# Three projections of a linear-attention layer by a seven-product scheme on quarters, one block ahead, on one Trainium2 core

## The chip, the core and the metric

The kernel runs on one core of one Trainium2 chip. The core has a matrix engine (TensorE, PE in the profile, with its weight loads as PEld), a vector engine (VectorE, DVE), a scalar engine (ScalarE, ACT), a general engine (GpSimd, POOL) and a queue that only issues DMAs (SyncE, SP). Each engine works through a list of instructions of its own, and they wait for each other by semaphores. Matrix products land in PSUM, which has eight banks of 128 partitions by 512 f32 numbers; everything else is in SBUF. The metric is device time in microseconds (us), lower is better. The time of the kernel before is 550.33 us, the median of three runs (549.09 to 550.42).

## The reference

The input x is 4 x 2048 tokens of 256 features in f32, so 8192 tokens. Two stages follow each other, each with a residual and a LayerNorm:

```python
Q = x @ W_q.T;  K = x @ W_k.T;  V = x @ W_v.T            # 256 x 256 weights
mask = where(i >= j, decay ** (i - j), 0)                # inside chunks of 32 tokens
S = einsum('bncd,bnkd->bnck', Qc, Kc) * mask             # per chunk, no softmax
O = einsum('bnck,bnkd->bncd', S, Vc)
x = layernorm(x + (sigmoid(x @ W_g.T) * O @ W_o.T + x))

gate = x @ wg.T;  up = x @ wu.T                          # int weights / 127, 768 hidden
x = layernorm(x + (silu(gate) * up) @ wd.T)
```

The attention part is computed in full f32. The FFN weights are integers from -127 to 127.

## The kernel before

The 8192 tokens are cut into 16 blocks of 512 (TB = 512, NB = 16). xT, the features by tokens, is loaded beside x, since a product needs its contraction on the partitions. `M = W_q.T W_k` is formed once (`make_m`), so that a block needs three projections of 256 x 256 before its attention, and none of K:

- `attn_y` (L314): y = M x, features by tokens, two PSUM banks, copied out by DVE (L327).
- `attn_gate` (L298): sigmoid(W_g x), features by tokens, two banks, ACT applies the sigmoid as it copies out (L311).
- `attn_v` (L330): v, tokens by features, two banks, copied out by ACT (L346).

Each of the three contracts 256 features in two steps (`ec`) and has two halves of output, so it is made of eight products of quarters. `attn_scores` (L351) forms y.T x in squares of 64 tokens and DVE multiplies the mask in (L369). `attn_values` (L374) multiplies v with the scores, and DVE multiplies the gate in (L387). `attn_out` (L421) projects back with W_o (the `pa` products, L406), adds 2x, and normalizes on DVE: `moments` (L264, L265), a square root on ACT (`root`, L273), then one pass over the tile (L288). The result h carries a factor of 2^23.

The FFN gets about f32 precision from two faster products: h is split into a high part in a reduced f32 type (`hT_hi`) and a low part in f16 (`hT_lo`). The integers are exact in both types; `integers` (L214) casts them on ACT into `fg_hi`, `fg_lo` and so on. `ffn_up` (L492) goes through hidden chunks `hc` of 128: eight products of 512 tokens into two banks (fg, fu), a sigmoid on ACT (L510), two multiplications on DVE (L512, L514), a cast to `u_hi` on ACT (L521), and the low part `u_lo` on POOL (L522). `ffn_down` (L524) makes the `fdn` products from `u_hi` and `u_lo`, and `finish` normalizes and stores.

h has to be transposed before the FFN. In the loop this is done off TensorE: `move_h` (L454) transposes squares of 32 on DVE (L461) and moves them with 16 DMAs on SP (L467); `split_h` (L475) then makes the high part on ACT (L484) and the low part on DVE (L485). The first and the last block are transposed on TensorE (`transpose_h`).

The loop runs over b = 0 to 13. One pass does the FFN of block b and the attention of block n = b + 2, and moves h of block b + 1. In source order a pass is: y, gate and v of n; scores; `move_h`; FFN chunks 0 to 2; values; `split_h`; chunks 3 to 5; `attn_out`; `ffn_down` and `finish`. Blocks 0 and 1 are done ahead of the loop, with y of block 2; the FFN of blocks 14 and 15 comes after it.

The order on each engine is set by a planner: it takes instructions in source order, but lets a later one pass when the earlier ones are not ready by its own cost estimates. `tc.keep_in_program_order` ties an instruction to its place. PSUM is one pool of eight banks (`bank`), and a bank comes free when its last reader is done. SBUF pools have a fixed number of buffers for each tag; `acts` has nine of `u_hi`.

Of the kernel before, what the change touches and what calls it, by code (L numbers as in the profile page):

```python
# [46 lines left out]
SQ = 32  # L50
TB = 512
NG = TB // P
SCALE = 1.0 / 127.0
EXACT = 128.0
H_UP = 2.0**23
# [6 lines left out]
def kernel(  # L62
# [28 lines left out]
    moved = ctx.enter_context(tc.tile_pool(name="moved", bufs=1))  # L91

    acts = ctx.enter_context(tc.tile_pool(name="acts", bufs=H // P + 3))
    small = ctx.enter_context(tc.tile_pool(name="small", bufs=8))
    psum = ctx.enter_context(tc.tile_pool(name="psum", bufs=8, space=bass.MemoryType.PSUM))

    def bank(name):
        return psum.tile([P, TB], F32, tag="ps", name=name)
# [36 lines left out]
    xns[0] = load_xn(0)  # L135
    if NB > 1:
        xns[1] = load_xn(1)
    ffn_int = [
        load_w(nc.sync, w, name)
        for w, name in ((ffn_gT, "fg_int"), (ffn_uT, "fu_int"), (ffn_dT, "fd_int"))  # L140
    ]


# [67 lines left out]
        nc.gpsimd.memset(sT, 0.0)  # L211


    def integers(w_int, name, dtype):  # L214
        name = f"{name}_{'hi' if dtype == F32R else 'lo'}"
        t = const.tile(list(w_int.shape), dtype, tag=name, name=name)
        tc.keep_in_program_order(nc.scalar.copy(t, w_int))
        return t


    halves = [
        (w_int, slice(i * w_int.shape[1] // 2, (i + 1) * w_int.shape[1] // 2))
        for w_int in ffn_int
        for i in range(2)
    ]
    top = const.tile([P, len(halves)], F32, tag="top", name="top")

    def look_up(i):
        w_int, ks = halves[i]
        reduced = nc.vector.tensor_reduce(  # L230
            top[:, i : i + 1],
            w_int[:, ks, :].rearrange("p k n -> p (k n)"),
            mybir.AxisListType.X,
            ALU.max,
            apply_absolute_value=True,
        )
        tc.keep_in_program_order(reduced)

    def count_wide():

        wide = const.tile([P, len(halves)], F32, tag="wide", name="wide")
        nc.vector.tensor_scalar(wide, top, EXACT, None, ALU.is_gt)
        ones = const.tile([P, 1], F32, tag="ones", name="ones")
        nc.vector.memset(ones, 1.0)
        pw = bank("pw")
        nc.tensor.matmul(pw[:1, : len(halves)], lhsT=ones, rhs=wide, start=True, stop=True)
        count = const.tile([1, 1], F32, tag="count", name="count")
        nc.vector.tensor_reduce(count, pw[:1, : len(halves)], mybir.AxisListType.X, ALU.add)
        n_wide = const.tile([1, 1], I32, tag="n_wide", name="n_wide")
        nc.vector.tensor_copy(n_wide, count)  # L250
        return n_wide
# [27 lines left out]
    def layer_norm(dst, r, name, on_r=1.0, on_dst=1.0):  # L279
# [7 lines left out]
        for g in range(NG):  # L287
# [6 lines left out]
                ALU.mult,  # L294
            )


    def attn_gate(b):  # L298
        xt = xTs[b]
# [90 lines left out]
    def back_terms(g, parts, ws):  # L390


        pairs = list(zip(parts, ws))[:: -1 if g % 2 else 1]
        return [(part[k], w[:, k, :]) for part, w in pairs for k in range(len(part))]

    def project_back(b, parts, ws, finish, name):

# [17 lines left out]
    def chunked(t):  # L415
        return [t[:, k, :] for k in range(t.shape[1])]
# [4 lines left out]
    def attn_out(b, goT, up=H_UP):  # L421
        xn = xns.pop(b)
        r = norm.tile([P, NG, D], F32, tag="h", name=f"h_{b}")

        def residual(gs, pb):

            nc.vector.scalar_tensor_tensor(
                flat(r, gs), flat(xn, gs), 2.0, pb, ALU.mult, ALU.add
            )

        project_back(b, (chunked(goT),), (wo,), residual, "pa")
        layer_norm(r, r, f"a{b}", on_dst=up)
        return r

# [40 lines left out]
    def split_h(b, hT):  # L475
        hi = work.tile([P, KD, TB], F32R, tag="hT_hi", name=f"hT_hi_{b}")
        lo = work.tile([P, KD, TB], F16, tag="hT_lo", name=f"hT_lo_{b}")
        for dc in range(KD):
            whole = hT[:, dc, :, :].rearrange("p q (g t) -> p g q t", g=NG)
            in_order = [  # L480
                part[:, dc, :].rearrange("p (g q t) -> p g q t", g=NG, q=NQ)
                for part in (hi, lo)
            ]
            tc.keep_in_program_order(nc.scalar.copy(in_order[0], whole))  # L484
            rest = nc.vector.tensor_tensor(  # L485
                in_order[1], whole, in_order[0].bitcast(F32), ALU.subtract
            )
            tc.keep_in_program_order(rest)
        return hi, lo


# [32 lines left out]
    def ffn_down(b, uT, h):  # L524
        r = work.tile([P, NG, D], F32, tag="r2", name=f"r2_{b}")

        def residual(gs, pb):

            nc.vector.scalar_tensor_tensor(
                flat(r, gs), pb, SCALE**3 / U_UP * H_UP, flat(h, gs), ALU.mult, ALU.add  # L530
            )

        project_back(b, uT, fd, residual, "fdn")
        return r

    def store(b, r, start=None):
# [23 lines left out]
    if second:  # L560
        sT_second = attn_scores(second, ys.pop(second))
    hs[first] = attn_out(first, goT, 1 if NB == 1 else H_UP)
    fg, fu = (
        [integers(w, name, dtype) for dtype in (F32R, F16)]
        for w, name in zip(ffn_int, ("fg", "fu"))
    )
    if second:
        goT = attn_values(second, sT_second, v_second, sg_second)
    if NB > 2:
        xTs[2] = load_xT(2)  # L570
        ys[2] = attn_y(2)
    if second:
        hs[second] = attn_out(second, goT, 1 if NB == 2 else H_UP)
    fd = [integers(ffn_int[2], "fd", dtype) for dtype in (F32R, F16)]
    hTs[first] = transpose_h(first, hs[first], 1 if NB == 1 else H_UP)


    half = range(KH // 2), range(KH // 2, KH)
    looked = 0
    for b in range(NB - 2):  # L580
        n = b + 2
        if n not in xTs:
            xTs[n] = load_xT(n)
        xns[n] = load_xn(n)
        hT = hTs.pop(b)
        uT = [], []
        yT = ys.pop(n) if n in ys else attn_y(n)
        sg, v = attn_gate(n), attn_v(n)
        sT = attn_scores(n, yT)
        moving = move_h(b + 1, hs[b + 1])  # L590
        ffn_up(b, hT, uT, half[0])
        goT = attn_values(n, sT, v, sg)
        hTs[b + 1] = split_h(b + 1, moving)
        ffn_up(b, hT, uT, half[1])
        hs[n] = attn_out(n, goT, 1 if n == NB - 1 else H_UP)
        finish(b, ffn_down(b, uT, hs.pop(b)))
        if looked < len(halves):
            look_up(looked)
            looked += 1
    for i in range(looked, len(halves)):  # L600
        look_up(i)


# [67 lines left out]

    for g in range(NG):
        pb = bank(f"fdn_{last}_{g}")[:, :D]
        terms = back_terms(g, uT_last, fd)
        for i, (part, w) in enumerate(terms):
            nc.tensor.matmul(
                pb,
                lhsT=part[:, g * P : (g + 1) * P],
                rhs=w,
                start=(i == 0),  # L680
                stop=(i == len(terms) - 1),
            )
        in_turn(
            nc.vector.scalar_tensor_tensor(
                r[:, g, :], pb, SCALE**3 / U_UP, hs[last][:, g, :], ALU.mult, ALU.add
            )
        )
        mv = moments(r, f"f{last}_{g}", [g], order=in_turn)
        if g == 0 and NB > 1:
            normalize(r_before, mv_before, std_before, f"f{last - 1}", H_UP)  # L690
            store(last - 1, r_before)
        std = root(mv, f"f{last}_{g}", groups=[g], order=in_turn)
        waiting.append((g, mv, std))
        if 0 < g < NG - 1:
            normalize_first()
        if g == NG - 2:
            normalize_first()
# [8 lines left out]
    def wide_block(start, weights):  # L706
# [18 lines left out]
        for hc in range(KH):  # L725
            pg = bank(f"fg_w_{hc}")
            pu = bank(f"fu_w_{hc}")
            for pb, w in ((pg, wide_g), (pu, wide_u)):
                for dc in range(KD):
                    nc.tensor.matmul(  # L730
                        pb,
                        lhsT=w[:, dc, hc * P : (hc + 1) * P],
                        rhs=hT[:, dc, :],
                        start=(dc == 0),
                        stop=(dc == KD - 1),
                    )
# [8 lines left out]
                flat(r, gs), pb, H_UP, flat(h, gs), ALU.mult, ALU.add  # L745
            )

        project_back("w", (uT,), (wide_d,), residual, "fdn")
        finish("w", r, start)

    wide_any = nc.values_load(
        n_wide, min_val=0, max_val=len(halves) * P, skip_runtime_bounds_check_because="a count"
    )
    with tc.If(wide_any > 0):
        weights = []
        for w_int in ffn_int:
            t = w_int.bitcast(F32)
            nc.vector.tensor_scalar(t, w_int, SCALE, None, ALU.mult)
            weights.append(t)
        with tc.For_i(0, NT, TB) as start:  # L760
            wide_block(start, weights)

# [41 lines left out]
```

## Time and profile before

The profile is of one execution with a span of 548.2 us, at a mean granted TensorE clock of 0.995.

| engine | busy us | share | instructions |
|---|---|---|---|
| PE | 538.8 | 98% | 3150 |
| PEld | 387.6 | 71% | 3150 |
| DVE | 385.3 | 70% | 956 |
| ACT | 231.3 | 42% | 383 |
| POOL | 128.6 | 23% | 122 |

PE, PEld, DVE, ACT and POOL are the engines; L12 is line 12 of the kernel. A group of instructions is named by its line, what it writes and what it reads. Ends of matrix products are modelled in the profile and overlap the next start, so their pace is read from start to start, or from the chain that ended last, which counts every stretch of time once. A product in full f32 shows as two records with a weight load each. "Idle before" is time in which an engine had nothing to do, with what ended it; it costs nothing on an engine that is not the bottleneck.

### The profile page before, as it was taken

The page shows a single profiled execution, that of the slowest core. Times are in us where ns is not written, and L with a number is a line of the kernel's source. Part 1 is how long each engine was busy: PE and PEld are TensorE (multiplying, and loading weights), DVE is VectorE, ACT ScalarE, POOL GpSimd, SP SyncE. Part 2 cuts the span into 40 slices and gives each one's busy share as a digit, 9 for nine tenths or more (in the row PEclk, how much of TensorE's full clock was granted, in tenths as well). Part 3 has the DMA queues.
Part 4 walks back from the last instruction along what each step waited for, and adds up shares of the span by engine and source line. Part 5 has one row for each costly group of instructions (what it writes and reads, how often), then busy time and mean ns, then how long its engine had stood idle before and what let it go on. Part 6 is the DMA issues. An engine that isn't in the chain of part 4 may idle for free.

```text
span 548.2 us, 8472 instructions
## 1 busy us (share of the span) xinstructions
PE 538.8 (98%) x3150; PEld 387.6 (71%) x3150; DVE 385.3 (70%) x956; ACT 231.3 (42%) x383; POOL 128.6 (23%) x122
## 2 busy tenths in 40 slices
PE   8999999999999999999999999999999999999994
PEld 5677767767667686677857677676676867678793
DVE  4267784859768486794848758496784858848875
ACT  2217524336243352433435243452433425344745
POOL 2000412305022040321304022050221404123453
PEclk9999999999999999999999999999999999999997
DMA  7431214121221312214122231213213120020102
GB/s 256 168 113 50 67 45 110 39 71 45 89 66 39 84 54 77 58 42 112 40 64 52 70 85 39 74 43 94 62 39 93 62 62 16 8 71 1 38 2 80
DMA packets 41996, 36.77 MB, mean 67 GB/s; under 512 B 4576, under 2 KB 37344, under 8 KB 41952
## 3 DMA queue, kind: packets, MB, share of 16 engines
q1 hardware_dynamic: 40832, 35.15, 22.5%
q10 hardware_dynamic: 1088, 1.05, 0.6%
q8 instruction: 26, 0.43, 0.3%
q14 instruction: 18, 0.15, 0.1%
q0 software_dynamic: 32, 0.00, 0.0%
HBM read 20.45 MB, written 8.39 MB: 53 GB/s over the span
## 4 chain that ended last, share of the span: by engine, by line
PE 97%; DVE 1%; ACT 1%; issue 0%; POOL 0%; DVEq 0%
PE fg L502 16%; PE fu L502 16%; PE fdn L406 15%; PE pg L304 10%; PE pa L406 10%; PE pv L339 10%; PE py L320 10%; PE po L380 5%; PE ps L359 3%; PE pi L148 1%; ACT r L646 0%; PE pt L443 0%; PE pm L162 0%; ACT L273 0%; ACT rstd_f L273 0%
## 5 line engine op out<-in xcount | busy, mean ns | idle before, releaser
L522 POOL TENSOR_TENSOR u_lo<-u,u_hi 128x512 f16<-128x512 f32 (+1 forms) x102 | 123.9, 1216 | 409.5 <-ACT u_hi L521 405.0
L510 ACT ACTIVATE s<-fg 128x512 f32<-128x512 f32 (+1 forms) x102 | 58.1, 570 | 76.2 <-PE fg L502 76.1
L512 DVE SCALAR_TENSOR_TENSOR s<-fg,s 128x512 f32<-128x512 f32 (+1 forms) x102 | 66.7, 654 | 28.0 <-ACT s L510 27.8
L521 ACT CAST u_hi<-u 128x512 fp32r<-128x512 f32 (+1 forms) x102 | 60.4, 592 | 48.8 <-DVE u L514 48.3
L514 DVE TENSOR_TENSOR u<-fu,s 128x512 f32<-128x512 f32 (+1 forms) x102 | 67.1, 660 | 13.8 <-POOL u_lo L522 1.1
L502 PE MATMUL fg<-hT_hi,fg_hi 128*128 128x512 f32 (+1 forms) x204 | 71.5, 431 | 0.0
L369 DVE TENSOR_TENSOR sT<-ps,mask 64x256 f32<-64x256 f32 x32 | 13.5, 422 | 78.5 <-PE ps L359 78.2
L502 PE MATMUL fu<-hT_hi,fu_hi 128*128 128x512 f32 (+1 forms) x204 | 61.4, 382 | 0.0
L502 PE MATMUL fg<-hT_lo,fg_lo 128*128 128x512 f16 (+1 forms) x204 | 58.9, 369 | 0.0
L304 PE MATMUL pg<-xT,wg 128*128 128x512 f32 x128 | 58.2, 598 | 0.0
L339 PEld LDWEIGHTS pv<-wv,xT 128*128 128x128 f32 x256 | 48.6, 190 | 13.4 <-issue 7.7
L502 PE MATMUL fu<-hT_lo,fu_lo 128*128 128x512 f16 (+1 forms) x204 | 58.1, 366 | 0.0
L406 PE MATMUL pa<-wo,goT 128*128 128x256 f32 x256 | 58.0, 379 | 0.0
L339 PE MATMUL pv<-wv,xT 128*128 128x256 f32 x256 | 57.9, 379 | 0.0
L320 PE MATMUL py<-xT,m_sb 128*128 128x512 f32 x128 | 57.6, 593 | 0.0
L406 PE MATMUL fdn<-fd_hi,u_hi 128*128 128x256 f32 x360 | 55.2, 295 | 0.0
L406 PEld LDWEIGHTS pa<-wo,goT 128*128 128x128 f32 x256 | 48.5, 190 | 7.6 <-DVE rstd_a L286 0.2
L406 PEld LDWEIGHTS fdn<-fd_hi,u_hi 128*128 128x128 f32 x360 | 46.6, 189 | 1.1
L304 PEld LDWEIGHTS pg<-xT,wg 128*128 128x128 f32 x128 | 24.4, 192 | 31.1 <-issue 28.9
L406 PE MATMUL fdn<-fd_lo,u_lo 128*128 128x256 f16 x360 | 44.5, 273 | 0.0
L502 PEld LDWEIGHTS fg<-hT_hi,fg_hi 128*128 128x128 f32 x204 | 36.6, 189 | 10.3
L502 PEld LDWEIGHTS fu<-hT_hi,fu_hi 128*128 128x128 f32 x204 | 37.5, 188 | 7.8
(91 smaller groups left out, 612.6 us busy)
## 6 DMA issues: line engine op xcount, KB each, us to landing
x<-in_x_dram SPq DMA_DIRECT2D x16, 512.0 KB, 3.5
xT<-in_xT_dram SPq DMA_DIRECT2D x15, 512.0 KB, 3.8
out_dram<-r SPq DMA_DIRECT2D x15, 512.0 KB, 3.3
hT<-sq SPq DMA_DIRECT2D x224, 32.0 KB, 1.9
fg_int<-in_ffn_gT_dram SPq DMA_DIRECT2D x1, 768.0 KB, 9.5
fu_int<-in_ffn_uT_dram SPq DMA_DIRECT2D x1, 768.0 KB, 10.9
fd_int<-in_ffn_dT_dram SPq DMA_DIRECT2D x1, 768.0 KB, 10.4
xT<-in_xT_dram SPq DMA_DIRECT2D x2, 256.0 KB, 4.2
```

The lines of the kernel that those rows point to most:

```text
L304: nc.tensor.matmul(pg, lhsT=wg[:, ec, dc * P : (dc + 1) * P], rhs=xt[:, ec, :], start=(ec == 0), stop=(ec == KD - 1),)
L320: nc.tensor.matmul(py, lhsT=m_sb[:, ec, fc * P : (fc + 1) * P], rhs=xt[:, ec, :], start=(ec == 0), stop=(ec == KD - 1),)
L339: nc.tensor.matmul(pv[:, j * D : (j + 1) * D], lhsT=xt[:, ec, g * P : (g + 1) * P], rhs=wv[:, ec, :], start=(ec == 0), stop=(ec == KD - 1),)
L359: nc.tensor.matmul(ps[rows, g, :], lhsT=xt[:, fc, tokens], rhs=yT[:, fc, tokens], start=(fc == 0), stop=(fc == KD - 1),)
L380: nc.tensor.matmul(po[:, cols], lhsT=v[:, g, dc * P : (dc + 1) * P], rhs=sT[:, cols], start=True, stop=True,)
L406: nc.tensor.matmul(pb[:, j * D : (j + 1) * D], lhsT=part[:, g * P : (g + 1) * P], rhs=w, start=(i == 0), stop=(i == len(terms) - 1),)
L502: nc.tensor.matmul(pb, lhsT=w[kind][:, dc, hc * P : (hc + 1) * P], rhs=hT[kind][:, dc, cols], start=(kind == kinds[0] and dc == 0), stop=( ...
L510: nc.scalar.activation(s, pg, AF.Sigmoid, scale=SCALE / H_UP)
L512: nc.vector.scalar_tensor_tensor(s, pg, U_UP / H_UP**2, s, ALU.mult, ALU.mult)
L514: nc.vector.tensor_tensor(u, pu, s, ALU.mult)
L521: nc.scalar.copy(hi, u)
L522: nc.gpsimd.tensor_tensor(lo, u, hi.bitcast(F32), ALU.subtract)
```

## The change

For y, gate and v of blocks 3 to 15 the eight products of quarters are replaced by seven (a scheme of the Strassen and Winograd kind). The weight is cut into quarters of 128 x 128, the block's xT into quarters of 128 features x 256 tokens. `weight_sums` forms five sums of weight quarters on POOL once for each of the three weights; `token_sums` forms four sums of token quarters on POOL once for each block, used by all three projections.

`seven` works in two parts. The first part makes products 1, 5, 7 and 6 into four banks (half of each is used). ACT copies 1, 5 and 7 to SBUF, DVE adds 6 and the copy of 1 to `u`, and POOL adds the copies of 5 and 7 to `p57`. The second part, called later, adds products 2, 3 and 4 onto the banks of 1, 5 and 7, and forms the four quarters of the result: one by ACT, two by DVE (bank plus `u`), one by POOL (`p57` plus `u`). For the gate, ACT applies the sigmoid to the first quarter as it copies, and to the others in place afterwards. For v the token quarters are the stationary operand, in groups of 128 tokens.

In the loop a pass now makes the three projections of block m = b + 3, one block ahead, with a piece of the FFN between the parts:

```diff
-        yT = ys.pop(n) if n in ys else attn_y(n)
-        sg, v = attn_gate(n), attn_v(n)
+        yT, v, sg = ahead.pop(n)
+        ffn_up(b, hT, uT, range(0, 2))
         sT = attn_scores(n, yT)
+        if m is not None and m + 1 < NB:
+            xTs[m + 1] = load_xT(m + 1)
         moving = move_h(b + 1, hs[b + 1])
-        ffn_up(b, hT, uT, half[0])
+        ffn_up(b, hT, uT, range(2, 3))
+        v_rest = y_rest = g_rest = nothing
+        if m is not None:
+            v_next, v_rest = split_v(m, x_sums[m])
+        ffn_up(b, hT, uT, range(3, 4))
+        v_rest()
         goT = attn_values(n, sT, v, sg)
+        if m is not None:
+            y_next, y_rest = split_y(m, x_sums[m])
+        ffn_up(b, hT, uT, range(4, 5))
+        y_rest()
         hTs[b + 1] = split_h(b + 1, moving)
-        ffn_up(b, hT, uT, half[1])
+        ffn_up(b, hT, uT, range(5, KH))
+        if m is not None:
+            sg_next, g_rest = split_gate(m, x_sums.pop(m))
         hs[n] = attn_out(n, goT, 1 if n == NB - 1 else H_UP)
+        g_rest()
+        if m is not None:
+            ahead[m] = y_next, v_next, sg_next
+            if m + 1 < NB:
+                x_sums[m + 1] = token_sums(xTs[m + 1], f"x_{m + 1}")
         finish(b, ffn_down(b, uT, hs.pop(b)))
```

The core of the scheme:

```diff
+        banks = {i: bank(f"p{i}_{name}")[:, :HB] for i in (1, 5, 7, 6)}
+        p = {}
+        for i, pb in banks.items():
+            product(i, pb, True)
+            if i != 6:
+                p[i] = part(f"p{i}")
+                nc.scalar.copy(p[i], pb)
+        u = part("p6")
+        nc.vector.tensor_tensor(u, banks[6], p[1], ALU.add)
+        p57 = part("p57")
+        nc.gpsimd.tensor_tensor(p57, p[5], p[7], ALU.add)
+
+        def others():
+            for i, onto in ((2, 1), (3, 5), (4, 7)):
+                product(i, banks[onto], False)
+            c11, c12, c21, c22 = (quarter(i, j) for i in range(2) for j in range(2))
+            nc.scalar.activation(c11, shaped(banks[1], c11), func)
+            nc.vector.tensor_tensor(c12, shaped(banks[5], c12), shaped(u, c12), ALU.add)
+            nc.vector.tensor_tensor(c21, shaped(banks[7], c21), shaped(u, c21), ALU.add)
+            nc.gpsimd.tensor_tensor(c22, shaped(p57, c22), shaped(u, c22), ALU.add)
```

The other parts of the change:

- The low part of h in `split_h` goes from DVE to POOL, and is no longer tied to its place:

```diff
-            rest = nc.vector.tensor_tensor(
+            nc.gpsimd.tensor_tensor(
                 in_order[1], whole, in_order[0].bitcast(F32), ALU.subtract
             )
-            tc.keep_in_program_order(rest)
```

- y, gate and v of block 2 are made ahead of the loop by the old functions: v directly after y, gate after `attn_out` of block 1 and the casts of `fd`. Then come the weight sums, the load of xT and the token sums of block 3, and the transposes of h of block 0.
- The integer weights are loaded in nine pieces of 128 x 512, which lie in the nine `u_hi` buffers of the pool `acts`, and no longer in three tiles of their own. ACT casts them piece by piece, 18 casts in place of six. `look_up`, the check of the largest weight, reads the cast high parts. The branch for weights over 127, which this input doesn't take, loads them anew.

## The prediction

> **What bounds the kernel now.** I read the page's busy line and chain first, then the chain of one steady loop pass in order of time, then the windows of two passes, then the waits.
>
> The page:
>
> ```profile
> PE 538.8 (98%) x3150; PEld 387.6 (71%) x3150; DVE 385.3 (70%) x956; ACT 231.3 (42%) x383; POOL 128.6 (23%) x122
> ...
> PE 97%; DVE 1%; ACT 1%; issue 0%; POOL 0%; DVEq 0%
> ...
> L522 POOL TENSOR_TENSOR u_lo<-u,u_hi 128x512 f16<-128x512 f32 (+1 forms) x102 | 123.9, 1216 | 409.5 <-ACT u_hi L521 405.0
> ```
>
> 97% of the chain is TensorE. A busy PE need not be PE at its peak, so I looked at start-to-start times. The chain of one pass (start, us, what):
>
> ```profile
> 241.13 3.43 PE py L320 x8
> 244.56 3.44 PE pg L304 x8
> 248.00 3.45 PE pv L339 x16
> 251.45 1.08 PE ps L359 x32
> 252.53 0.66 PE fg L502 x2
> 253.19 0.47 PE fu L502 x2
> ...
> 258.15 1.78 PE po L380 x16
> 259.93 0.43 PE fg L502 x2
> ...
> 265.32 3.45 PE pa L406 x16
> 268.78 5.51 PE fdn L406 x48
> ```
>
> Each group begins where the last one ends: no gap. The three products that the change touches (y, gate, v) are 3.43 + 3.44 + 3.45 = 10.32 us of a pass. Windows of two passes (us, PE, PEld, DVE, ACT, POOL busy, clock, DMA share, GB/s):
>
> ```profile
> 240.97:274.13 33.16, 33.16 (x194) 23.69 (x193) 24.36 (x59) 13.44 (x22) 7.68 (x6) 1.00 0.23 64
> 274.13:307.25 33.12, 33.12 (x195) 23.69 (x194) 23.39 (x57) 13.44 (x22) 7.70 (x6) 1.00 0.23 65
> ```
>
> A pass is 33.1 us of PE at full clock, and every other engine has at least 8.8 us spare. PE's own waits are one line, before any work (PE pi on DVE idle, 1.5 us). So PE time taken out comes off the span, as long as no other engine's order makes PE wait.
>
> [...] py 3.43/8 = 429 ns for 512 columns, pv 3.45/16 = 216 ns for 256, po 1.78/16 = 111 ns for 128[...] Trace: u_lo takes 1280 ns at 512 elements and 731 at 256, 2.1 ns an element; and the one large DVE operation with two SBUF inputs, the low part of h, is bimodal (min/median/max):
>
> ```profile
> L485 DVE TENSOR_TENSOR hT_lo<-hT,hT_hi x28: 677/688/1375, 63.0 to 494.4; 128x512 f16<-128x512 f32 x28
> ```
>
> [...]
>
> **The change part by part.** It works on blocks 3 to 15, so 13 passes; block 2 keeps the old products and only moves ahead of the loop.
>
> *Seven products.* A quarter product is 128x128x256. For y and gate it is 2 records of 256 columns: 7 x 2 x 0.2156 = 3.02 us for 3.43 or 3.44. For v the weights move, in 2 groups of 128 columns: 7 x 2 x 2 = 28 records of 128 columns, at po's 0.111: 3.12 us for 3.45. Saved: 0.41 + 0.42 + 0.33 = 1.16 us a pass, 13 x 1.16 = 15.1 us. All of it is on the path. Bounds for v: 2.99 us at the pace of 256 columns; the other end stands under the rivals.
>
> *Two parts with an FFN chunk between.* New changes of kind on PE. In the chain the first fg pair after f32 products costs 0.66 against 0.47 when it begins with the high part (after ps) and 0.43 when it begins with the low part (after po). Chunk 3 and 5 begin low, chunk 4 high; scores now stand ahead of chunk 2 (high) as they stood ahead of chunk 0. So one more, 0.19 us a pass: 2.5 us (from 0 to 5).
>
> *Sums and evacuation.* Nearest rows are those at 128x256: ACT 380 to 405 ns, DVE 414 to 423, POOL 731. Per pass ACT gains 9 copies, 3 c11 and two sigmoids in place (0.38 + 0.60) and loses 4 at 0.59: +3.3 us, and 0 to 2 table loads more, since gate's sigmoids now stand between the two square roots: 13.4 becomes 16.7 to 19.3. DVE gains 9 x 0.42 = 3.8 and loses two y copies (1.3) and the low part of h (2.0): 24.4 becomes 24.9. POOL gains 4 token sums, 3 p57, 3 c22 (10 x 0.73) and two low parts (about 1.3 each; above that if the rearranged read costs more): 7.7 becomes 17.6. All are below the new pass of about 32.2 us, so throughput costs nothing; PE's work beside them hides them, if the waits below fit.
>
> *The waits.* New: the second part (p2 onto bank 1, p3 onto 5, p4 onto 7) waits for ACT's copies. For v the four first products take 4 x 0.445 = 1.78 us and chunk 3 follows with 1.83. p1's copy has from 0.45 to 3.6 us, p7's from 1.3 to 4.5. ACT must do in that time the copies (1.2), s and u_hi of chunk 2 (1.2), perhaps the u_hi before (0.6): 3.0 us. It fits with 0.6 us or more. For gate the cover is pa, 3.45 us. Queued behind the copies are s and u_hi of the next chunk; FFN banks wait for those.
>
> *Banks.* Three of eight are held through a chunk (1.8 + 1.8 + 1.3 us and the evacuation), so 5 remain for chunks (2 each, free 1.1 and 1.9 us after the chunk) and po. On DVE, the slack that stood beside y, gate and v (idle 4.9 us ahead of sT) is now later. In the first 8 us of a pass DVE owes the rest of the FFN norm (about 4.2), four transposes (1.7), sT (0.86), and s and u of three chunks (4.1), some 11 us; the backlog of 3 us leaves chunk 2's banks held until po, when 8 are wanted. I take 0.15 us a pass for both waits, 2 us (0 to 13).
>
> *h moved one place.* The transposed h goes out in DMAs whose issue is long (start, us; SP's queue):
>
> ```profile
> 244.91 1.87 SPq L467 DMA_DIRECT2D hT<-sq  x3
> 246.83 0.59 SPq L537 DMA_DIRECT2D out_dram<-r  x1
> 247.46 8.53 SPq L467 DMA_DIRECT2D hT<-sq  x13
> 256.09 0.53 SPq L109 DMA_DIRECT2D xT<-in_xT_dram  x1
> ```
>
> 16 issues are 10.4 us, 1.9 more to landing: 17 us after the pass begins. The load of xT now stands ahead of them (0.5 us), and waits for the scores at 4.8 us if SP keeps that order: landing at 17.5 to 18.5. split_h stands after y's second part, at about 18.3 us by PE. So ACT arrives as the data does; behind it wait s of chunk 5 and gate's copies, with pa to cover. The low part on POOL (2.6 us) is then done by 22 to 25 us; h is wanted at 32. Nothing, up to 0.5 us a pass.
>
> *Ahead of the loop.* Gate and v of block 2 stand ahead of the transposes of h, which came at 44.71; ffn_up(0) now follows these directly and waits for ACT, which has fd's casts (6 x 0.54), sigmoids and a table load nearby. 1 us (0 to 4). 15 POOL weight sums at about 0.4 us lie beside it. Casts in 18 pieces for 6: 9.7 for 8.2 us of ACT, hidden by the f32 products. Integer loads are 9 of 256 KB for 3 of 768 KB, used 25 us after landing.
>
> *Last pass.* It has no products of a block ahead: PE 22.8 us, DVE about 21. 1 us (0 to 4).
>
> Sum: -15.1 + 2.5 + 2 + 1 + 1 = -8.6; 548.2 - 8.6 = 539.6 us of span. The median of the three runs, 550.33, is 2.1 above that span: **541.7 us**.
>
> **The rivals.**
> 1. *PE waits for copies or banks* half a microsecond more each pass: 13 x 0.5 = 6.5, 548.2 us: still just faster or level. For: ACT's u_hi waits for DVE in 68 places already (48.3 us), and what is listed behind it waits too. Against: the margins above, and ACT at most 60% busy.
> 2. *ACT's queue held at the high part of h*, the slower end. If the transposes run after sT (about 9.7 us) instead of in DVE's gaps, h lands at about 22 us; s of chunk 5 and gate's copies wait 3 us behind it, u_lo of chunk 5 comes at 27.4 plus POOL's queue, and fdn stands from 26.6. 1.5 us of PE a pass: 541.7 + 19.5 = 561. It decides from about 0.8 us a pass ((552 - 541.7)/13). Against: in this trace the transposes run at 1 to 4 us, interleaved with the norm, though the source has them after the scores.
> 3. *v is limited by weight loads*: 28 f32 loads of 190 ns one after another are 5.3 us, 1.9 more than now, 13 x 2.2 = 28 us above the forecast. po speaks against it: same loads at 192 ns, 16 records in 1.78 us. I give it almost nothing.
> 4. *The change doesn't do what it says*: an eighth of 10.32 us is 1.29, and 1.16 remains; the record count shows it.
>
> **How the numbers follow.** Forecast, its own range 537.5 to 545.5: 0.60. Better than it (no waits, no switch cost: 548.2 - 15.1 + 2.1 = 535 is the floor): 0.05. Rival 1, up to 548.7: 0.13; its end that reaches no change, 548.7 to 552.0 (0.3% either way, about what a measurement can tell): 0.08. Rivals 2 and 3, slower: 0.14. So faster 0.78, same 0.08, slower 0.14. The range of 8 in 10 runs from 536.5 to 551.
>
> **What would show it.** Right: passes of 32.3 us; v's first and second part 1.78 and 1.33 us; 14, 14 and 28 records; PE at 97% of the chain; POOL near 250 us; low part of h near 1.3 us. Wrong: PE waits on ACT copies ahead of the second parts, or on DVE for a bank, of over 0.8 us a pass; hT_hi waiting for the DMA of hT; v's records at 120 ns or more.

## The result and the profile after

The kernel after takes **545.58 us** (median of four runs, 545.20 to 547.08), beside 550.38 for the kernel before (four runs, 549.09 to 551.12). The ratio is 0.992, with a 95% interval of 0.9894 to 0.9947: faster by 0.8%. The forecast of 541.7 was 3.9 us too low. The 545.58 lies 0.08 us above the forecast's own range (537.5 to 545.5) and inside the range of 8 in 10 (536.5 to 551). The kernel before, run beside the later experiments too, had medians of 550.34 (experiments 1 to 4) and 550.43 (5 to 8), so times of different experiments can be compared. The profiled execution of the kernel after was the longest of its four: a span of 545.3 us, where the other three have 543.4 to 544.0. The sums below are made from its trace and so end on that span.

The page after, with the lines that answer to those shown of before:

```profile
PE 527.8 (97%) x3462; PEld 419.8 (77%) x3462; DVE 387.7 (71%) x1019; ACT 306.9 (56%) x551; POOL 261.1 (48%) x295
...
PEclk9999799999999999999999999999999999999998
...
PE 90%; DVE 3%; ACT 2%; SPq 1%; POOL 1%; issue 1%; DMA 0%; DVEq 0%; ACTq 0%
...
L677 POOL TENSOR_TENSOR u_lo<-u,u_hi 128x512 f16<-128x512 f32 (+1 forms) x102 | 123.7, 1214 | 173.4 <-ACT u_hi L676 172.3
L641 POOL TENSOR_TENSOR hT_lo<-hT,hT_hi 128x512 f16<-128x512 f32 x28 | 35.3, 1282 | 27.6 <-ACT hT_hi L640 27.6
```

TensorE's busy time fell by 11.0 us (538.8 to 527.8), but its share of the chain fell from 97% to 90%. The chain now leaves TensorE at two more places: from 48.8 to 56.9, ahead of the loop, and from 468.9 to 497.0, where it follows h of block 14 (its norm, its DMAs, its two parts) to the end of the last pass. Most of that second stretch lies beside busy TensorE, so the share is no measure of time lost; the waits are. The row of granted clock has a single 7, early on. PE's waits (engine, line, awaited; us in total, times, longest); the line left out is that of before, pi on DVE:

```profile
PE fg L657 <- ACT hT_hi L602: 3.8, 1, 3.8
PE fdn L562 <- POOL u_lo L677: 1.8, 1, 1.8
...
PE fdn L562 <- ACT u_hi L676: 0.6, 1, 0.6
```

Each new wait occurs once, not thirteen times. The first stands at the start of the first FFN chunk of pass 0, the other two in the last pass, which makes no products of a block ahead. The chain of a pass that does, from 283.78 to 315.77 (start, us, what; 288.46 follows the scores):

```profile
288.46 0.66 PE fg L657 x2
...
290.48 1.78 PE p_v L380 x16
292.26 0.43 PE fg L657 x2
...
294.04 1.34 PE p_v L380 x12
...
297.17 1.73 PE p_y L364 x8
298.89 0.46 PE fg L657 x2
...
300.70 1.29 PE p_y L364 x6
...
303.79 1.73 PE p_g L364 x8
...
308.97 1.29 PE p_g L364 x6
```

v is 1.78 + 1.34, y and the gate are 1.73 + 1.29 each: 9.16 us for 10.32 before, 1.16 less. The second parts of v and y begin where the FFN chunk ends, that of the gate where `pa` ends. Windows of two passes, and of the place with the 7 (us; PE, PEld, DVE, ACT, POOL busy; clock; DMA share; GB/s):

```profile
91.74:123.75 32.01, 32.01 (x218) 26.07 (x217) 24.35 (x63) 18.97 (x34) 17.20 (x18) 1.00 0.24 66
123.75:155.76 32.01, 32.01 (x217) 26.07 (x217) 24.46 (x63) 19.09 (x34) 17.18 (x18) 1.00 0.23 67
56.80:62.40 5.60, 5.51 (x13) 2.69 (x14) 2.67 (x4) 1.12 (x3) 0.00 (x0) 0.51 0.24 51
```

A pass is 32.01 us for 33.13. The third window holds chunk 0 of the first block's FFN and most of chunk 1 (13 products; a chunk has eight): TensorE is busy all through it, at half clock.

**Where the time went**, from the spans (548.2 to 545.3):

| stretch | before | after | difference |
|---|---|---|---|
| ahead of the loop and pass 0, to the end of the first `fdn`, without y, gate and v of block 3 | 75.47 | 91.74 - 9.16 = 82.58 | +7.1 |
| the twelve passes that follow, and the 1.16 us saved in the thirteenth | 12 x 33.13 | 12 x 32.01 | -13.4 - 1.2 = -14.6 |
| last pass, b = 13, without products of a block ahead | 33.15 - 10.32 = 22.83 | 25.66 | +2.8 |
| from there to the end | | | +1.9 |

The last line is in the stores. From the end of the last pass to the end of DVE's last operation both traces have the same 39.02 us; then the issues of the last four stores took 3.45 us for 2.84, and from issue to landing they took 3.0 for 1.8 (median). From the end of DVE's last operation to the end of the span are 2.9 us before, 4.9 after and 5.0 in experiment 1 (533.40 to 538.4); no run shows why. The sum is -2.8 for -2.9.

**The +7.1.** ACT's timeline ahead of the loop, after (start, us, instruction, count, in brackets the idle time before it):

```profile
50.54 0.30 ACT L305 ACTIVATE rstd_a<-mv_a,eps 128x4 f32<-128x4 f32 x1 [4.11 <-DVE mv_a L297]
50.75 1.64 ACT L253 CAST fd_hi<-fd_int 128x512 fp32r<-128x512 int32 x3
...
53.97 1.28 ACT L467 ACT_TABLE_LOAD   x1
55.26 1.08 ACT L467 ACTIVATE sg<-pg 128x512 f32<-128x512 f32 x2
56.23 1.09 ACT L602 ACTIVATE hT_hi<-pt 128x512 fp32r<-128x512 f32 x2
```

TensorE's transposes of h of block 0 begin at 52.05 and last a microsecond. Their evacuation `hT_hi` stands on ACT behind the square root of block 1's norm, six casts of fd, a table load and two sigmoids of the gate. ACT idles 4.11 us ahead of that square root. Before, `hT_hi` ran ahead of it:

```profile
45.35 1.08 ACT L446 ACTIVATE hT_hi<-pt 128x512 fp32r<-128x512 f32 x2 [1.08 <-PE pt L443]
47.17 0.30 ACT L273 ACTIVATE rstd_a<-mv_a,eps 128x4 f32<-128x4 f32 x1 [0.73 <-DVE mv_a L265]
```

So TensorE waits 3.8 us, and what follows runs at half clock (0.51 in the window from 56.80). Some 0.4 us of the 7.1 lie earlier, in the first projection of the kernel (4.68 us in the chain for 4.22).

**The +2.8.** ACT's and then PE's timeline in the last pass:

```profile
492.57 1.14 ACT L640 CAST hT_hi<-hT 128x512 fp32r<-128x512 f32 x2 [2.16 <-DMA hT<-sq]
```

```profile
494.28 0.38 PE L562 MATMUL fdn<-fd_hi,u_hi 128*128 128x256 f32 x1 [0.62 <-ACT u_hi L676]
...
497.04 0.94 PE L562 MATMUL fdn<-fd_lo,u_lo 128*128 128x256 f16 x7 [1.81 <-POOL u_lo L677]
```

ACT stands at the high part of h until the DMA of hT has landed; `u_hi` of the last chunk is behind it (at 493.62), and on POOL `u_lo` behind two low parts of h (2.5 us). In a pass with products this is hidden: in the one shown ACT waited 0.47 us for the landing, at 302.03, and TensorE still had pa and the gate's second part to do.

### The profile page after: what moved, and what is told of

Its sections match the earlier page's. It is cut to its first block, busy times and chain, and to the rows that moved or that the text cites. A ratio compares the mean times of both kernels' runs of the same rounds, so it can differ in the third digit from the quotient of the medians.

```text
span 545.3 us, 9852 instructions
## 1 busy us (share of the span) xinstructions
PE 527.8 (97%) x3462; PEld 419.8 (77%) x3462; DVE 387.7 (71%) x1019; ACT 306.9 (56%) x551; POOL 261.1 (48%) x295
## 4 chain that ended last, share of the span: by engine, by line
PE 90%; DVE 3%; ACT 2%; SPq 1%; POOL 1%; issue 1%; DMA 0%; DVEq 0%; ACTq 0%
PE fg L657 16%; PE fu L657 15%; PE fdn L562 14%; PE pa L562 10%; PE p_v L380 7%; PE p_y L364 7%; PE p_g L364 7%; PE po L536 5%; PE ps L515 3%; PE py L476 2%; PE pv L495 2%; PE pg L460 1%; SPq L623 1%; PE pi L178 1%; ACT L305 0%
## 5 line engine op out<-in xcount | busy, mean ns | idle before, releaser
L657 PE MATMUL fg<-hT_hi,fg_hi 128*128 128x512 f32 (+1 forms) x204 | 74.7, 447 | 3.8 <-ACT hT_hi L602 3.8
L641 POOL TENSOR_TENSOR hT_lo<-hT,hT_hi 128x512 f16<-128x512 f32 x28 | 35.3, 1282 | 27.6 <-ACT hT_hi L640 27.6
L562 PEld LDWEIGHTS <-u_lo 128*128 128x128 f16 x360 | 32.7, 98 | 6.9 <-POOL u_lo L677 2.1
L657 PEld LDWEIGHTS <-fu_lo 128*128 128x128 f16 x204 | 20.1, 99 | 22.2 <-DVE sT L525 1.2
L583 DVE SCALAR_TENSOR_TENSOR h<-x,pa 128x512 f32<-128x512 f32 x32 | 22.0, 688 | 20.6 <-PE pa L562 20.0
L657 PEld LDWEIGHTS <-fg_lo 128*128 128x128 f16 x204 | 16.0, 99 | 19.8 <-issue 13.3
```

The lines of the kernel that those rows point to most:

```text
L562: nc.tensor.matmul(pb[:, j * D : (j + 1) * D], lhsT=part[:, g * P : (g + 1) * P], rhs=w, start=(i == 0), stop=(i == len(terms) - 1),)
L641: nc.gpsimd.tensor_tensor(in_order[1], whole, in_order[0].bitcast(F32), ALU.subtract)
L657: nc.tensor.matmul(pb, lhsT=w[kind][:, dc, hc * P : (hc + 1) * P], rhs=hT[kind][:, dc, cols], start=(kind == kinds[0] and dc == 0), stop=( ...
```

## The experiments

**The theory**: the seven products pay in full in every pass, and 9 to 10 us are given back at two places outside them, each by one instruction's place in ACT's order. **The rivals**: the time ahead of the loop is lost to more than the order; the saving in the passes comes from the new order and not from seven for eight; the low part of h on GpSimd, or the chunks between the parts, matter.

### 1. The transposes of block 0 earlier

```diff
+    hTs[first] = transpose_h(first, hs[first], ...)
     if second:
         hs[second] = attn_out(second, goT, ...)
...
-    hTs[first] = transpose_h(first, hs[first], ...)
```

> One edit to the changed kernel: the TensorE transposes of h of block 0 stand ahead of attn_out of block 1, as early as they came in the kernel before, so that the high part of h of block 0 does not stand behind the fd casts and the gate's sigmoids on ACT. Theory A (the gain is lost at the two ends, the larger piece ahead of pass 0: 3.8 us of PE waiting on ACT hT_hi and then chunk 0 at half clock, some 2.8 us): the wait and the half clock go, 545.6 - 6.6 = 539 us. Rival B (the casts in 18 pieces and the sums on POOL are what fills the stage ahead of the loop, the place of the transposes does not matter): PE finds another wait there, 545 us.

Measured: 541.06 us (539.84 to 541.55, five runs), ratio to before 0.9833 (0.9813 to 0.9853), 4.5 us under the kernel after. The high part of h is now ahead of the square root on ACT:

```profile
46.00 1.08 ACT L602 ACTIVATE hT_hi<-pt 128x512 fp32r<-128x512 f32 x2
```

and its line is gone from PE's waits, while the other three of the kernel after stay as they were. The granted clock is 1.00 from 38 to 92 us, and the first `fdn` starts at 79.55 for 86.23, 6.7 us earlier: the wait of 3.8, and 2.9 that is mostly the slow chunks 0 and 1. The medians differ by less (4.5). The profiled execution of the kernel after had the lowest mean clock of its four (0.989 for 0.992 to 0.993), and in the traces of experiments 2 and 4, behind the same wait of 3.8, the half clock lasted 3.41 us for 6.83, so in other executions it may have cost less; no trace of them exists. The place is shown; the rival falls: the 18 casts and the sums on GpSimd are all still there.

### 2. The high part of h behind `attn_out`, in the last pass alone

```diff
-        hTs[b + 1] = split_h(b + 1, moving)
+        if m is not None:
+            hTs[b + 1] = split_h(b + 1, moving)
...
         hs[n] = attn_out(n, goT, ...)
+        if m is None:
+            hTs[b + 1] = split_h(b + 1, moving)
```

> One edit to the changed kernel: in the last pass alone, which has no products of a block ahead, split_h stands after attn_out. Theory A (ACT stands 2.2 us at hT_hi for the DMA of hT, and u_hi and u_lo of chunk 5 come late behind the two halves of h on ACT and POOL, so fdn waits 0.6 + 1.8 us): these waits go, 545.6 - 2.5 = 543.1 us. Rival C (the last pass is bound by DVE, 21 us of work in 23): the wait moves to DVE u, less than 0.8 us gained.

Measured: 543.39 us (542.52 to 543.68, four runs), ratio 0.9871 (0.9850 to 0.9893), 2.2 us under the kernel after. Both waits of `fdn` are gone, and the wait of 3.8 stays. The second place is shown too.

### 3. Both

The two edits together.

> Both edits. Theory A: they add up, 545.6 - 6.6 - 2.5 = 536.5 us, the kernel before less 13 x 1.13 us and some 0.8 us more. Rivals B or C: 543 to 545 us.

Measured: **537.19 us** (537.04 to 537.75, five runs), ratio 0.9767 (0.9750 to 0.9785). PE's waits are again the one line of before the change, pi on DVE. Two moved calls are worth 8.4 us, nearly twice what the whole change had brought; this version is 2.3% faster than the kernel before and 1.5% faster than the one after. The two gains alone sum to 6.7; half clock for 3.41 us, as behind the wait that is left in experiment 2, costs by estimate the other 1.7, but no run isolates it.

### 4. Eight products in the new order

```diff
-            v_next, v_rest = split_v(m, x_sums[m])
+            v_next = attn_v(m)
...
-            y_next, y_rest = split_y(m, x_sums[m])
+            y_next = attn_y(m)
...
-            sg_next, g_rest = split_gate(m, x_sums.pop(m))
+            sg_next = attn_gate(m)
```

The sums of weights and tokens are gone as well.

> The changed kernel with the old eight products and evacuations (one bank pair, one copy) in the place of the first parts of the seven; order, one block ahead, integer pieces and the low part on POOL stay; no sums. Theory A (the seven products save 1.13 us a pass in full and nothing else in a pass costs): passes of 33.1 us, 545.6 + 13 x 1.13 = 560.3 us. Rival D (the order costs part of what the seven products save, by waits for copies, so without them passes would be under 33.1): 552 to 557 us.

Measured: 558.88 us (557.75 to 559.25, four runs), ratio 1.0152 (1.0129 to 1.0175). The new order, with the integer pieces and the low part on GpSimd that stay in, makes the kernel 8.5 us slower by itself. Two of its `fdn` groups in the chain:

```profile
119.60 5.49 PE fdn L562 x48
...
152.74 5.49 PE fdn L562 x48
```

A pass is 33.14 us, that of before, and the waits of 3.8 and 1.8 are there as in the kernel after. So the whole saving of a pass is seven for eight, and the losses don't come from the seven products. Seven for eight is worth 13.3 us by the medians (558.88 - 545.58), 14.7 by the passes.

### 5. TensorE kept busy during the wait

```diff
     hTs[first] = transpose_h(first, hs[first], ...)
+    pf = bank("pf")
+    for _ in range(5):
+        nc.tensor.matmul(pf, lhsT=idle[:, :P], rhs=idle, start=True, stop=True)
```

Five products of zeros, which nothing reads, fill the wait of 3.8 us; the order is that of the kernel after.

> The changed kernel with five matrix products of zeros right after the transposes of h of block 0, 10 records of about 0.43 us in the 3.8 us in which PE waits for hT_hi; nothing else moves. Theory A splits the loss ahead of pass 0 into the wait and, after it, chunk 0 at about half clock (5.5 us for 1.84 in the profile). With PE fed, the wait stays, as work, and chunk 0 should run at full clock: pass 0 begins some 0.5 us later and chunk 0 takes 1.9 us, 545.6 - 1.5 to 3 = 543 us. If the half clock is not from the wait: 546 us.

Measured: 546.25 us (544.02 to 546.73, six runs), ratio 0.9914 (0.9897 to 0.9931): nothing gained, against an expected 1.5 to 3. It is the number expected for the opposite case, that the half clock doesn't come from the wait, but the trace says otherwise. The windows of its trace, of chunks 0 and 1 and of the last pass's `fdn`, with its longer wait there:

```profile
56.00:62.00 6.00, 6.00 (x52) 3.49 (x51) 3.54 (x6) 2.83 (x6) 0.42 (x1) 1.00 0.25 52
...
495.00:500.50 5.50, 5.38 (x34) 4.84 (x35) 2.39 (x8) 0.23 (x1) 0.06 (x1) 0.69 0.00 0
...
PE fdn L562 <- ACT u_hi L676: 1.2, 1, 1.2
```

The first step went as expected: chunk 0 runs at full clock (1.00 in the first window), and pass 0 ends 2.5 us earlier (89.22 for 91.74). But in this execution the half clock came in the last pass, behind the waits of 1.2 and 1.8 (0.69 in the second window; the last section sets it beside the kernel after): the 37 `fdn` from 495 on took 5.96 us for the 4.39 of the kernel after, 1.6 more. The wait of 1.2 is 0.6 longer than in the kernel after, as ACT waited 2.77 us for h instead of 2.16. These two take back 2.2 of the 2.5; 0.3 is left, and 0.3 is what the spans differ by (545.0 for 545.3). How often each stretch slows over many executions stays open.

### 6. The second parts directly behind the first

On the version with both edits (537.19):

```diff
             v_next, v_rest = split_v(m, x_sums[m])
-        ffn_up(b, hT, uT, range(3, 4))
         v_rest()
+        ffn_up(b, hT, uT, range(3, 4))
...
-        ffn_up(b, hT, uT, range(4, 5))
         y_rest()
+        ffn_up(b, hT, uT, range(4, 5))
...
+        g_rest()
         hs[n] = attn_out(n, goT, ...)
-        g_rest()
```

> The kernel with both edits (537.2 us), and the second part of each of the seven-product groups directly after the first, the FFN chunk after both. Theory A (the copies are 0.4 us each and ACT is free when they come, so the order 1, 5, 7, 6 is cover in itself): the second part waits 0 to 0.3 us a pass, 537 to 541 us. Rival (the chunk between is what hides the copies): each of v and y waits 0.8 us or more for ACT, passes of 33.6, 557 us.

Measured: 541.41 us (540.82 to 542.24, four runs), ratio 0.9831 (0.9815 to 0.9847) for 0.9767. The chain shows v as one piece:

```profile
287.66 3.12 PE p_v L380 x28
```

The products cost the same: 3.12 here, and 3.02 for y. Between the starts of the first and the thirteenth `fdn` a pass takes 32.38 us on average for 32.00, 0.4 more: 0.5 in passes 1 to 5, 1.3 in pass 6 and 0.1 in passes 7 to 12. In passes 1 to 6 DVE also has a step of the check of the weights (`look_up`, 0.94 us); that it makes the difference is not shown. Part of the 0.4 is in weight loads that wait for ACT's copies (the gate's are shown; y's are 2.6 us in 6 waits, all in passes 1 to 6):

```profile
PEld p_g L364 <- ACT p_g L407: 3.6, 13, 0.3
```

The work between the parts is worth 4.2 us. It isn't the whole condition of the change: with the two edits, the kernel without it still beats the one before (541.41 for 550.43).

### 7. The low part of h on DVE

Also on the version with both edits:

```diff
-            nc.gpsimd.tensor_tensor(
+            rest = nc.vector.tensor_tensor(
                 in_order[1], whole, in_order[0].bitcast(F32), ALU.subtract
             )
+            tc.keep_in_program_order(rest)
```

> The kernel with both edits (537.2 us), the low part of h back on DVE and tied to its place, as in the kernel before. Theory A (PE waits for nothing in a pass and DVE has 7 us spare): passes of 32.0 us, 537 us, up to 1 us either way. Rival (that move is needed, since DVE owes 2 to 2.75 us more there, ahead of s and u of chunks 4 and 5 and of the copies' sums): passes of 32.5 us or more, 543 us.

Measured: 536.86 us (536.57 to 537.18, four runs), ratio 0.9754 (0.9739 to 0.9770) for 0.9767 (0.9750 to 0.9785): no difference. Its summary of the tile (min/median/max in ns, first and last start):

```profile
L641 DVE TENSOR_TENSOR hT_lo<-hT,hT_hi x28: 681/684/1768, 71.3 to 491.3; 128x512 f16<-128x512 f32 x28
```

TensorE waits for neither engine, and the move to GpSimd carries nothing of the gain.

### 8. h landing later

Six more DMAs of 32 KB, to a spare tile, ahead of the 16 of `move_h` in every pass, on the version with both edits:

```diff
+        for i in range(6):
+            nc.sync.dma_start(spare[...], sq[...])
         for q in range(NQ):
             for j in range(NQ):
                 nc.sync.dma_start(...)
```

> The kernel with both edits (537.2 us), and in every pass six DMAs of the same kind more (to a tile that nobody reads) ahead of the sixteen that move h: 6 x 0.65 = 3.9 us later for h. This is the place of the prediction's second rival, at its price. In a pass of the kernel with both edits u_lo of chunk 5 ends 2.2 us before fdn wants it, and ACT and POOL take the halves of h ahead of it: 3.9 - 2.2 = 1.7 us of PE waiting in fdn a pass, 13 x 1.7, 559 us. If h has the slack that the prediction gave it (up to 0.5 us lost): 537 to 544 us.

Measured: 561.95 us (561.62 to 564.17, four runs), ratio 1.0219 (1.0197 to 1.0242): 24.8 us over the version with both edits, 1.9 a pass. The size is near the expected one, but the delay was larger than planned: h landed 23.2 us into a pass for 17.8 (mean of passes 1 to 12), 5.4 later instead of 3.9. The place is not the expected one. PE's waits:

```profile
PE p_v L380 <- DVE s L676: 15.1, 11, 1.8
PE fdn L562 <- POOL u_lo L686: 4.0, 7, 1.2
```

ACT stands at h in every pass (3.06 us ahead of the cast at 244.90), as rival 2 had it, but TensorE pays only 4.0 us of it at `fdn`. The larger part, 15.1 us, is paid in the next pass, where the first part of v waits for a bank that DVE holds. (By start-to-start times v's first part is 18.2 us longer over the run and `fdn` 4.9, nearly all of the 24.8.) Timelines of DVE and POOL there:

```profile
261.01 2.43 DVE L320 TENSOR_SCALAR r<-r,mv_f,rstd_f 128x256 f32<-128x256 f32 x4
```

```profile
262.01 1.28 POOL L686 TENSOR_TENSOR u_lo<-u,u_hi 128x512 f16<-128x512 f32 x1 [8.31 <-ACT u_hi L685]
```

The same four in the version with both edits:

```profile
281.08 1.38 DVE L320 TENSOR_SCALAR r<-r,mv_f,rstd_f 128x256 f32<-128x256 f32 x4
```

DVE reaches the last step of the FFN's norm 5.7 us after `fdn` has ended (255.27) for 4.6 (276.51), and there it meets the `u_lo` of a chunk on GpSimd. One of the four instructions then takes up to 1452 ns for 410. Over the run `r` sums to 30.8 us for 19.4, about 1.04 in each of 11 passes, and p_v waits 11 times. In the one pass of twelve where the four took 1.38 us (at 158.71) it doesn't wait. So a delay of h costs two things: rival 2's own wait, the smaller, and a norm that takes longer beside `u_lo`. That the meeting lengthens `r` is read from the overlap; no run moved `u_lo` away.

## Why the prediction was right, and where it was off

The measured 545.58 lies in the stretch that the prediction gave to rival 1, waits for copies or banks in every pass, and these did not come. The mechanism was right, the costs around it were not: those put too high in the loop offset about half of what was missed at its two ends. That the number is off by only 3.9 us is in part luck.

- **Seven products**: right to the number. 9.16 us for the forecast 10.32 - 1.16, parts of v of 1.78 and 1.34 (forecast 1.78 and 1.33). Experiment 4 shows that nothing else makes the passes shorter. Rivals 3 and 4 fall. (The lower bound for v, 2.99, should read 3.02: 14 records of 256 columns at 0.2156. Nothing hangs on it.)
- **Two parts, 2.5 us for changes of kind**: mis-sized, it is 0.5. Without the products a pass takes 22.85 us (32.01 - 9.16) for 22.81 before, 0.04 times 13. The step read the 0.66 of the fg pair behind the scores as the price of starting with the high part. The pass shown has fg pairs behind p_v and p_y at 0.43 and 0.46; the 0.66 follows the scores alone, and there is one of it in a pass before and after.
- **Waits for copies and banks, 2 us; rival 1**: nothing. The copies fit beside the chunks, and experiment 6 gives the value of that room: 0.4 us a pass on average.
- **h one place later**: the high part ran 18.25 us into the pass (302.03 - 283.78; forecast 17.5 to 18.5), ACT waited 0.47 us for it, TensorE not at all. A sign of being wrong that the prediction named, `hT_hi` waiting for the DMA of hT, is there, but it cost TensorE something only once, in the last pass; rival 2 did not come in the others. Experiment 8 brings a time of its size, 561.95 for 561, but with h 5.4 us late and mostly by another way.
- **Ahead of the loop, 1 us (0 to 4)**: 7.1, the step that failed by the most. It named the place and the right queue, ACT with fd's casts, sigmoids and a table load "nearby", but did not add them up: 3.1 + 1.3 + 1.0 us stand ahead of the first half of `hT_hi`, and the square root at their head waits for DVE. The wait is 3.8, and with the half clock behind it, which no step had, it makes most of the 7.1: experiment 1 takes 6.7 away.
- **Last pass, 1 us (0 to 4)**: 2.8, of which the two waits are 2.4. Its sum counted PE and DVE; the landing of h, worked out a few lines above for the other passes, was not set against a pass that is 9 us shorter.
- **What would show it**: passes of 32.0 for 32.3, PE 90% of the chain for 97%, POOL 261 us for 250, the low part of h 1282 ns for 1.3 us.

The sum of the prediction, on the trace: -15.1 + 0.5 + 0 + 7.1 + 2.8 = -4.7, and 1.9 of late stores make -2.8. The forecast of -8.6 had 4.0 us in costs that didn't come, and was 7.9 short at the two ends of the loop. The stores are in no step. By medians the kernel gained 4.8.

## What to carry to other kernels

When a loop is re-ordered, what the loop body gains is the easy part: walk through the stages that run once, ahead of it and in its last pass, with the same list of "who stands ahead of this instruction on its engine", and add up the durations. A wait that is hidden in the loop shows in the pass whose covering work has been taken away. A wait of TensorE can cost more than its length: behind the wait of 3.8 us here, 5.6 us of products ran at a granted clock of 0.51.

## What the runs showed of the hardware

**The clock after a wait.** In the traces of the kernels before and after, the granted clock, from its first record on, changes only at whole multiples of 3.413 us: one clock lasts 535.89 us in the kernel before (157 multiples), and 47.79, 6.83 and 477.87 us in the kernel after (14, 2 and 140). Where half clock begins against the wait of 3.8 differs from one execution to the next: 1.48 us ahead of its end in the kernel after (55.41 and 56.89), 1.31 and 1.49 us behind it in experiments 2 and 4 (57.98 and 56.67, 58.10 and 56.61). The dip of the kernel after is two stretches of 3.413 us long (55.41 to 62.24), those of experiments 2, 4 and 5 one (57.98 to 61.39, 58.10 to 61.51, 495.1 to 498.5). The edges of the three experiments are worked out from the clock of their windows, to about 0.02 us in 2 and 4 and 0.05 in 5. How long TensorE idled, by its records, in such a stretch:

| place | idle us in the stretch, or in two in turn | clock behind it |
|---|---|---|
| kernel after, ahead of pass 0, wait of 3.8 | 2.33 | half |
| experiment 2, the same wait | 1.70, 2.11 | full, half |
| experiment 4, the same wait | 1.88, 1.92 | full, half |
| kernel after, last pass, waits of 0.6 and 1.8 | 1.13, 1.31 | full, full |
| experiment 5, last pass, waits of 1.2 and 1.8 | 0.5, 2.5 | full, half |
| experiment 8, waits at `p_v` in 11 passes | at most 1.8 | full (`po` behind it 1.79 us) |

In these rows, and in every other stretch at full clock in the traces of before and after, 1.88 us or less had full clock behind it and 1.92 or more half clock (2.03 at the end of the kernel before, 3.41 at that of the kernel after). The waits of 1.2 and 1.8 in experiment 5 fall mostly into one stretch and half clock follows; those of 0.6 and 1.8 in the kernel after are spread over two and none does. The same pair of waits was not measured in both positions.

**DVE beside GpSimd.** Two operations of DVE show a long form beside the `u_lo` of GpSimd. The low part of h takes 677 to 692 ns in 15 of its 28 instances in the kernel before and 1365 to 1375 in 13. All 13 started 0.48 us after a `u_lo` and ended 0.55 us after it had ended. Of the 15 short ones one (at 63.04) overlaps a `u_lo`, for its last 0.07 us, and the others none. In experiment 7 the longest is 1768 ns (median 684). The last step of the FFN's norm takes up to 1452 ns in experiment 8 (median 410), and at most 415 in the version with both edits. In the pass shown of experiment 8 its four instructions end at 263.44, 0.15 us after the `u_lo` that started at 262.01. What holds them up is not shown. On GpSimd the low part of h takes 1272 to 1411 ns (experiment 3), with no such tail.
